# A 4x4 Hadamard convolution as the last of four layers: both directions transformed on the data, the two output halves in two strips of array columns, the data planes shared by VectorE and GpSimd

## The chip, the cores and the metric

One Trainium2 chip, one core. The kernel computes four convolution layers in one launch. The metric is the time of one execution on the device in microseconds (us); lower is better. Engines are named as the profile names them: PE is TensorE (PEld its weight loads), DVE is VectorE, ACT is ScalarE, POOL is GpSimd, SP is SyncE, which here only issues transfers.

## The reference, cut to what matters

All data is float32, `x` has the shape (2, 128, 128, 128): batch, channels, rows, columns. Each layer normalises its input in 32 groups of channels and adds its result to the input. The change touches the last layer only:

```python
_HMT  = [[1,1,1,1],[1,-1,1,-1],[1,1,-1,-1],[1,-1,-1,1]];  _HMT2 = _HMT[[1,0,2,3], :]
_IH = (_HMT / 4)[1:3, :];  _IH2 = (_HMT2.T / 4)[1:3, :]

def _L3_conv_ref(x, weight, bias):                 # weight: (128, 128, 4, 4)
    patches = _extract_patches(x)                  # 4x4 patches at stride 2, padding 1
    hmt1 = einsum('up,bchwpq,qv->bchwuv', _H,  patches, _H)
    hmt2 = einsum('pu,bchwpq,qv->bchwuv', _H2, patches, _H2)
    m1 = einsum('bchwuv,ocuv->bohwuv', hmt1, weight[:64])
    m2 = einsum('bchwuv,ocuv->bohwuv', hmt2, weight[64:])
    o1 = einsum('au,bohwuv,cv->bohwac', _IH,  m1, _IH)
    o2 = einsum('au,bohwuv,cv->bohwac', _IH2, m2, _IH2)
    ...                                            # a, c: place in a 2x2 block of the output
    return out + bias

x = x + _L3_conv_ref(_gn(x), weight, bias)
```

Each 4x4 patch is turned into 16 sums and differences (u, v) of its taps, each is multiplied with its own 128 x 64 weights for the first and the second half of the output channels (with different matrices for the two halves), and sums and differences of the 16 products make a 2x2 block of the output.

## The kernel before

The data stays in SBUF for the whole kernel as `res`, channels on partitions. The earlier layers are an attention along one direction (layer 0, which ends in a stage that merges its results into `res`), four scans over lines (layer 1), an offsets' convolution and a deformable convolution (layer 2). They run before `layer3` and are the same in both kernels.

`layer3` first loads the weights (`ta`, on ScalarE's queue), transforms them by four adds of 128x1024 on VectorE (L1673 and L1674), and writes them, scaled and with signs, into `weff`: 32 small scalings on VectorE (L1682) for the first 64 output channels, and 32 on ScalarE (L1686) for the other 64. `group_norm` makes scale and shift.

Then it works through 32 blocks of eight rows (2 images x 16 blocks). For each block:

- `normalise`: two ScalarE operations write the normalised even and odd columns, with one row more above and below, into `col0` and `col1`, each 10 rows x 65 columns. GpSimd clears the edge columns and, at the edges of the image, a row.
- `transform`: eight VectorE adds of 128x640 make four planes `x3` (10 rows x 64) of sums and differences of four neighbouring columns. Only one direction is transformed on the data; the other one lies in the weights.
- `multiply`: 4 planes x 2 outputs c x 4 row taps q = 32 matmuls with 128x128 weights and 256 moving columns, into four PSUM tiles m0 to m3, each with two buffers. The profile shows a float32 matmul as two instructions, so 64 of them a block.
- `finish`: ScalarE takes m3 (with the bias) and m2 out of PSUM into `t` and `s`; four VectorE adds of 64x512 add m0 and m1; two of 128x512 make the sum and the difference of `t` and `s`, and two more add the residual `res`; SyncE's queue then sends the block out.

The order of the work on TensorE, VectorE and ScalarE is written out by hand: the class `InOrder` wraps an engine, and what is issued through it keeps the order of the program. Such instructions all carry the helper's line in the profile, L81, so they are told apart by their tiles. Turn i multiplies block i, finishes block i - 1, normalises block i + 2 and transforms block i + 1. GpSimd isn't wrapped.

Other rows that the prediction names: the stage that merges layer 0 (VectorE and GpSimd each add 128x1024 pieces, `res<-te,res`), the last of layer 1's four scans (`ln`, `v`, `u`, `x1t`, with PSUM tiles `pl`), the addition of two sets of scan weights at L1035, a running sum on GpSimd at L183, and the offsets' convolution at L1234 (PSUM tile `ps_off`), whose inner loop is

```python
for k in range(9):
    for s in range(4):
        nc.tensor.matmul(ps[32 * s : 32 * s + 32], lhsT=woff[:, k, :], rhs=..., ...)
```

where the partitions of the output (32 s to 32 s + 31) say which strip of array columns works.

Of the kernel before, what the change touches and what calls it, by code (L numbers as in the profile page):

```python
# [7 lines left out]
F32 = mybir.dt.float32  # L8
I32 = mybir.dt.int32
AF = mybir.ActivationFunctionType  # L10
ALU = mybir.AluOpType
AX = mybir.AxisListType
PSUM = bass.MemoryType.PSUM
DRAM = bass.MemoryType.DRAM

P = 128
N = 2
S = 128
# [1633 lines left out]
def layer3(env, prm, res, st_gn, out):  # L1652

    nc, tc = env.nc, env.tc
    flip = (1, 0, 2, 3)
    RB = 8
    with ExitStack() as ctx:  # L1660
        cp = ctx.enter_context(tc.tile_pool(name="l3c", bufs=1))
        bias = cp.tile([P, 1], F32, name="bias3", tag="bias3")
        nc.scalar.dma_start(out=bias, in_=prm["b3"])
        weff = cp.tile([P, 4, 2, 4, P], F32, name="weff", tag="weff")
        with tc.tile_pool(name="l3w", bufs=1) as wp:
            ta = wp.tile([P, 16 * P], F32, name="ta", tag="ta")
            tb = wp.tile([P, 16 * P], F32, name="tb", tag="tb")
            nc.scalar.dma_start(out=ta, in_=prm["w3"])
            a, b = ta, tb
            for bit in range(2):  # L1670
                va = a.rearrange("p (h t k) -> p h t k", t=2, k=P << bit)
                vb = b.rearrange("p (h t k) -> p h t k", t=2, k=P << bit)
                nc.vector.tensor_tensor(vb[:, :, 0], va[:, :, 0], va[:, :, 1], ALU.add)  # L1673
                nc.vector.tensor_tensor(vb[:, :, 1], va[:, :, 0], va[:, :, 1], ALU.subtract)  # L1674
                a, b = b, a
            what = a.rearrange("p (u v o) -> p u v o", u=4, v=4)
            for u in range(4):
                for c in range(2):
                    for q in range(4):
                        to = weff[:, u, c, q, :]  # L1680
                        sign = (1, -1, 1, -1)[u]
                        nc.vector.tensor_scalar(  # L1682
                            to[:, 0:64], what[:, u, (c + 1) ^ q, 0:64], sign / 16, None, ALU.mult
                        )
                        sign = (-1, 1, 1, -1)[u] * (-1, 1)[c]
                        nc.scalar.mul(  # L1686
                            to[:, 64:128],
                            what[:, (0, 3, 2, 1)[u], (3, 2)[c] ^ flip[q], 64:128],
                            sign / 16,
                        )  # L1690

        sp = ctx.enter_context(tc.tile_pool(name="l3s", bufs=2))
        with tc.tile_pool(name="l3pn", bufs=1, space=PSUM) as pn:
            gs, gb = env.group_norm(cp, pn, st_gn, "l3")
        pp = ctx.enter_context(tc.tile_pool(name="l3ps", bufs=2, space=PSUM))
        pe, dve, act = (InOrder(tc, e) for e in (nc.tensor, nc.vector, nc.scalar))
        blocks = [(n, h) for n in range(N) for h in range(0, S, RB)]

        def normalise(i):

            n, h = blocks[i]
            lo, hi = max(0, h - 1), min(S, h + RB + 1)
            cols = [
                sp.tile([P, RB + 2, 65], F32, name=f"col{k}", tag=f"col{k}") for k in range(2)
            ]
            nc.gpsimd.memset(cols[0][:, :, 0:1], 0.0)  # L1706
            nc.gpsimd.memset(cols[1][:, :, 64:65], 0.0)  # L1707
            for k in range(2):
                if h == 0:
                    nc.gpsimd.memset(cols[k][:, 0, :], 0.0)  # L1710
                if h == S - RB:
                    nc.gpsimd.memset(cols[k][:, RB + 1, :], 0.0)
            rows = slice(lo - h + 1, hi - h + 1)
            for k in range(2):
                act.activation(
                    cols[k][:, rows, 1 - k : 65 - k],
                    res[n][:, lo:hi, 1 - k :: 2],
                    AF.Identity,
                    bias=gb[:, n : n + 1],
                    scale=gs[:, n : n + 1],  # L1720
                )
            return cols

        def transform(cols):

            x = sp.tile([P, 4, RB + 2, 64], F32, name="x3", tag="x3")
            t = sp.tile([P, 2, RB + 2, 64], F32, name="t3", tag="t3", bufs=1)
            for k, op in ((0, ALU.add), (2, ALU.subtract)):
                even, odd = x[:, k], t[:, k // 2]
                dve.tensor_tensor(even, cols[0][:, :, 0:64], cols[0][:, :, 1:65], op)  # L1730
                dve.tensor_tensor(odd, cols[1][:, :, 0:64], cols[1][:, :, 1:65], op)
                dve.tensor_tensor(x[:, k + 1], even, odd, ALU.subtract)
                dve.tensor_tensor(even, even, odd, ALU.add)
            return x

        def multiply(x):
            got = []
            for u in range(4):
                ps = pp.tile([P, 2, RB // 2, 64], F32, name=f"m{u}", tag=f"m{u}")
                for c in range(2):  # L1740
                    for q in range(4):
                        pe.matmul(
                            ps[:, c],
                            lhsT=weff[:, u, c, q, :],
                            rhs=x[:, u, q : q + RB - 1 : 2, :],
                            start=(q == 0),
                            stop=(q == 3),
                        )
                got.append(ps.rearrange("p c h w -> p (c h w)"))
            return got  # L1750

        def finish(i, m):

            n, h = blocks[i]
            t = sp.tile([P, 512], F32, name="t", tag="t")
            s = sp.tile([P, 512], F32, name="s", tag="s")
            act.activation(t, m[3], AF.Identity, bias=bias)
            act.copy(s, m[2])
            for half, k in ((slice(0, 64), (0, 1)), (slice(64, 128), (1, 0))):
                dve.tensor_tensor(t[half], m[k[0]][half], t[half], ALU.add)  # L1760
                dve.tensor_tensor(s[half], m[k[1]][half], s[half], ALU.add)
            ot = sp.tile([P, RB, S], F32, name="ot", tag="ot")
            o = ot.rearrange("p (h a) (w c) -> p a c h w", a=2, c=2)
            r = res[n][:, h : h + RB, :].rearrange("p (h a) (w c) -> p a c h w", a=2, c=2)
            tv = t.rearrange("p (c h w) -> p c h w", c=2, w=64)
            sv = s.rearrange("p (c h w) -> p c h w", c=2, w=64)
            for a, op in enumerate((ALU.add, ALU.subtract)):
                dve.tensor_tensor(o[:, a], tv, sv, op)
                dve.tensor_tensor(o[:, a], o[:, a], r[:, a], ALU.add)
            nc.sync.dma_start(out=out[n, :, h : h + RB, :], in_=ot)  # L1770

        count = len(blocks)
        cols = {0: normalise(0), 1: normalise(1)}
        xs = {0: transform(cols.pop(0))}
        ms = {}
        for i in range(count + 1):
            if i < count:
                ms[i] = multiply(xs.pop(i))
            if i >= 1:
                finish(i - 1, ms.pop(i - 1))  # L1780
            if i + 2 < count:
                cols[i + 2] = normalise(i + 2)
            if i + 1 < count:
                xs[i + 1] = transform(cols.pop(i + 1))

# [3 lines left out]
def program(ctx, tc, prm, out):  # L1791
# [32 lines left out]
    with tc.tile_pool(name="l1w", bufs=1) as wp:  # L1824
# [3 lines left out]
        layer1(env, prm, res, both, x1_d, st_gn[1], st_gn[0], first)  # L1828
    layer2(env, prm, res, mem, tables, st_gn[0], st_gn[1])
    layer3(env, prm, res, st_gn[1], out)  # L1830


# [127 lines left out]
```

## Time and profile before

| | |
|---|---|
| median of 3 runs | 5747.52 us (5745.45 to 5751.23) |
| the profiled execution | 5755.18 us, its span 5753.0 us |
| mean granted TensorE clock | 0.97 |
| PE busy | 5381.7 us (94%) |
| DVE busy | 3775.1 us (66%) |
| ACT busy | 2647.0 us (46%) |
| POOL busy | 1288.8 us (22%) |
| last layer: issue of its first load, first matmul, start of the last eviction | 5279.86, 5298.18, 5742.68 us |

How to read the rows: a group's row has the line, the engine, the operation, the tiles written and read, the shapes and the count; then the busy time in us and the mean length of one in ns; then the idle time of the engine just before these instructions, and what ended most of it. In a timeline a row begins with its start and length in us. Busy times of matmuls overlap, since the engine takes up the next before the last has ended; the pace is busy time by count. In a row of a tile the three numbers after the count are the shortest, the median and the longest in ns. A VectorE operation's length reaches a little into the next one's; the distance of two starts is its price in a stream.

### The profile page before, as it was taken

The page shows a single profiled execution, that of the slowest core. Times are in us where ns is not written, and L with a number is a line of the kernel's source. Part 1 is how long each engine was busy: PE and PEld are TensorE (multiplying, and loading weights), DVE is VectorE, ACT ScalarE, POOL GpSimd, SP SyncE. Part 2 cuts the span into 40 slices and gives each one's busy share as a digit, 9 for nine tenths or more (in the row PEclk, how much of TensorE's full clock was granted, in tenths as well). Part 3 has the DMA queues.
Part 4 walks back from the last instruction along what each step waited for, and adds up shares of the span by engine and source line. Part 5 has one row for each costly group of instructions (what it writes and reads, how often), then busy time and mean ns, then how long its engine had stood idle before and what let it go on. Part 6 is the DMA issues. An engine that isn't in the chain of part 4 may idle for free. (4 is left out here: it accounts for less than half of the span.)

```text
span 5753.0 us, 162512 instructions
## 1 busy us (share of the span) xinstructions
PE 5381.7 (94%) x67323; PEld 4838.1 (84%) x67323; DVE 3775.1 (66%) x7289; ACT 2647.0 (46%) x7928; POOL 1288.8 (22%) x983
## 2 busy tenths in 40 slices
PE   8997999999999708999999999997999999998999
PEld 8866888888888608999999999963999999998888
DVE  3645888888888765555555566643666666666887
ACT  1046989898888774442223320022333333333221
POOL 2113666666666530000000013310000000000000
PEclk9998999999999859999999999998999999999999
DMA  3243333333333491000000001125766677663001
GB/s 146 96 189 105 62 62 60 59 62 62 59 59 58 125 373 50 2 1 1 1 1 1 1 16 39 44 65 118 87 88 88 87 84 90 88 87 50 41 37 41
DMA packets 413668, 401.01 MB, mean 70 GB/s; under 512 B 63488, under 2 KB 368512, under 8 KB 402304
## 3 DMA queue, kind: packets, MB, share of 16 engines
q1 hardware_dynamic: 403856, 363.87, 30.9%
q10 hardware_dynamic: 9072, 26.64, 1.2%
q8 instruction: 541, 8.86, 0.7%
q14 instruction: 199, 1.63, 0.1%
HBM read 251.00 MB, written 139.37 MB: 68 GB/s over the span
## 5 line engine op out<-in xcount | busy, mean ns | idle before, releaser
L81 PE MATMUL pl<-ln,wl 128*128 128x128 f32 (+1 forms) x10160 | 1240.7, 276 | 7.4 <-DVE ln L81 7.2
L81 PEld LDWEIGHTS pl<-ln,wl 128*128 128x128 f32 x10160 | 1176.2, 190 | 18.3 <-DVE ln L81 4.4
L81 ACT ACTIVATE e<-e,mx 128x128 f32<-128x128 f32 x2048 | 793.4, 395 | 0.8 <-DVE mx L81 0.8
L81 ACT COPY sm<-ps_s 128x432 f32<-128x432 f32 (+1 forms) x768 | 318.3, 487 | 803.3 <-PE ps_s L81 803.3
L81 ACT COPY res<-ln 128x128 f32<-128x128 f32 x762 | 262.0, 344 | 720.4 <-DVE ln L81 720.4
L81 POOL TENSOR_TENSOR e<-e,total 128x1024 f32<-128x1024 f32 x256 | 485.9, 1898 | 478.1 <-DVE total L81 470.3
L81 DVE COPY s<-ps_w 100x1152 f32<-100x1152 f32 x256 | 346.5, 1354 | 307.1 <-PE ps_w L81 307.1
L81 PE MATMUL ps_s<-s,xw 100*128 100x144 f32 x4096 | 545.1, 286 | 0.2 <-ACT sm L81 0.2
L81 PE MATMUL po<-sm,wdef 128*128 128x256 f32 x2304 | 539.1, 379 | 0.0
L81 PE MATMUL pl<-ln,ws 128*128 128x128 f32 x4064 | 536.8, 273 | 0.0
L81 POOL COPY et<-et 128x1024 f32<-128x1024 f32 x256 | 516.1, 2016 | 35.7 <-DVE et L81 27.0
L81 PEld LDWEIGHTS ps_s<-s,xw 100*128 100x128 f32 x4096 | 517.1, 190 | 0.7 <-ACT sm L81 0.7
L81 DVE TENSOR_TENSOR v<-pl,c 128x128 f32<-128x128 f32 x508 | 148.2, 292 | 538.0 <-PE pl L81 538.0
L81 PEld LDWEIGHTS pl<-ln,ws 128*128 128x128 f32 x4064 | 494.5, 190 | 0.0
L81 ACT ACTIVATE r<-gen,alphas 128x1536 f32<-128x1536 f32 x256 | 394.9, 1543 | 174.2 <-PE gen L81 145.3
L81 POOL TENSOR_TENSOR res<-ln,x1t 128x128 f32<-128x128 f32 x256 | 134.4, 525 | 1485.1 <-DVE ln L81 1485.1
L81 PEld LDWEIGHTS po<-sm,wdef 128*128 128x128 f32 x2304 | 419.8, 190 | 47.6
L81 PE MATMUL m<-x,weff 128*128 128x256 f32 x2048 | 444.4, 380 | 14.8 <-DVE x L81 14.8
L81 PEld LDWEIGHTS m<-x,weff 128*128 128x128 f32 x2048 | 390.6, 191 | 68.3 <-issue 14.9
L1706 POOL MEMSET col<- 128x10 f32 x32 | 3.7, 116 | 1869.1 <-ACT weff L1686 1490.7
L81 ACT ACTIVATION_READ_ACCUMULATOR e<-e,mx 128x1 f32 x2048 | 396.7, 194 | 0.0
L81 DVE SCALAR_TENSOR_TENSOR ln<-v,res 128x128 f32<-128x128 f32 x1016 | 343.7, 338 | 49.2 <-DVE v L81 1.3
(225 smaller groups left out, 8806.6 us busy)
## 6 DMA issues: line engine op xcount, KB each, us to landing
xw<-px_d SPq DMA_DIRECT2D x1280, 80.0 KB
xa<-in_x SPq DMA_DIRECT2D x16, 1024.0 KB
v_d<-vs SPq DMA_DIRECT2D x16, 1024.0 KB
qb_d<-sb SPq DMA_DIRECT2D x16, 1024.0 KB
qa_d<-sa SPq DMA_DIRECT2D x8, 2048.0 KB
zz<-qb_d SPq DMA_DIRECT2D x1024, 16.0 KB
vt<-v_d SPq DMA_DIRECT2D x64, 256.0 KB
qk<-qa_d SPq DMA_DIRECT2D x256, 64.0 KB
```

The lines of the kernel that those rows point to most:

```text
L81: return lambda *a, **k: self.tc.keep_in_program_order(issue(*a, **k))
L1706: nc.gpsimd.memset(cols[0][:, :, 0:1], 0.0)
```

## The change

Both directions are now transformed on the data, separately for the two halves of the output channels, and each matmul has 64 output channels.

- Weights: ScalarE scales `ta` by 1/16 as a whole; VectorE makes `tb` and then `weff` by 16 adds of 128x256.
- `normalise`: the same; GpSimd's memsets keep the program's order now (`pool` is wrapped too).
- `second`, on GpSimd: planes for the second half: two adds of 650 elements (even and odd columns) into `a3`, two of 650 (even and odd rows) into `b3`.
- `first_columns`, on VectorE: four adds of 640 elements into `d3`. `first_rows`: four adds of 1024 elements into `q3`, three on VectorE and one on GpSimd.
- `multiply`: 2 x 2 x 2 x 2 products x 2 halves = 32 matmuls with 128x64 weights and 256 moving columns; the halves alternate, and write partitions 0 to 63 and 64 to 127 of one PSUM tile `m3` with three buffers.
- `combine`: ScalarE takes half of `m3` out of PSUM (two operations of 256 elements, one with the bias); VectorE adds and subtracts the other half in PSUM (two of 512 elements), then makes sums and differences of the result (two of 512) into `ot`.
- `finish`: GpSimd adds the residual (1024 elements); SyncE's queue sends the block out.
- Buffers: `a3`, `d3`, `c3` and `f3` have one, `b3`, `ot` and the columns two, `q3` four, which is one block's planes.
- Order: turn i multiplies block i; then finishes block i - 2 and makes the planes of block i + 1; then combines block i - 1 and normalises block i + 2.

The diff, cut to its core:

```diff
-        weff = cp.tile([P, 4, 2, 4, P], F32, name="weff", tag="weff")
+        weff = cp.tile([P, 4, 4, P], F32, name="weff", tag="weff")
...
+            nc.scalar.mul(ta, ta, 1.0 / 16)
+            def pairs(engine, to, w):
+                one, two = slice(0, H), slice(H, P)
...
+            pairs(nc.vector, lambda k, o: tb[:, k, :, o], lambda v, o: ta[:, :, v, o])
+            pairs(nc.vector, lambda k, o: weff[:, :, k, o], lambda u, o: tb[:, :, u, o])
...
-        pp = ctx.enter_context(tc.tile_pool(name="l3ps", bufs=2, space=PSUM))
-        pe, dve, act = (InOrder(tc, e) for e in (nc.tensor, nc.vector, nc.scalar))
+        pp = ctx.enter_context(tc.tile_pool(name="l3ps", bufs=3, space=PSUM))
+        pe, dve, act, pool = (
+            InOrder(tc, e) for e in (nc.tensor, nc.vector, nc.scalar, nc.gpsimd)
+        )
...
+        def second(cols):
+            even, odd = cols
+            a = sp.tile([P, 2, RB + 2, 65], F32, name="a3", tag="a3")
+            b = sp.tile([P, 2, 2, RB // 2 + 1, 65], F32, name="b3", tag="b3", bufs=2)
+            for k, op in enumerate((ALU.subtract, ALU.add)):
+                pool.tensor_tensor(a[:, k], even, odd, op)
+            for k, op in enumerate((ALU.subtract, ALU.add)):
+                pool.tensor_tensor(b[:, k], a[:, :, 0::2, :], a[:, :, 1::2, :], op)
+            return b
+
+        def first_columns(cols):
+            even, odd = cols
+            d = sp.tile([P, 4, RB + 2, H], F32, name="d3", tag="d3")
+            for k, op in enumerate((ALU.add, ALU.subtract)):
+                dve.tensor_tensor(d[:, 2 * k], odd[:, :, 0:H], even[:, :, 1:65], op)
+                dve.tensor_tensor(d[:, 2 * k + 1], even[:, :, 0:H], odd[:, :, 1:65], op)
+            return d
+
+        def first_rows(d, k):
+            q = sp.tile([P, 4, RB // 2, H], F32, name="q3", tag="q3", bufs=4)
+            lo, hi = ((1, 2), (0, 3))[k % 2]
+            (dve, dve, dve, pool)[k].tensor_tensor(
+                q,
+                d[:, :, lo : lo + RB - 1 : 2, :],
+                d[:, :, hi : hi + RB - 1 : 2, :],
+                ALU.add if k < 2 else ALU.subtract,
+            )
+            return q
+
+        def multiply(qs, b):
+            ps = pp.tile([P, 2, 2, RB // 2, H], F32, name="m3", tag="m3")
+            for r in range(2):
                 for c in range(2):
...
+                    for x in range(2):
+                        for y in range(2):
+                            for half in range(2):
+                                part = slice(H * half, H * half + H)
+                                if half == 0:
+                                    rhs = qs[2 * r + x][:, 2 * c + y]
+                                else:
+                                    rhs = b[:, r, c, x : x + RB // 2, y : y + H]
+                                pe.matmul(
+                                    ps[part, r, c],
+                                    lhsT=weff[:, 2 * r + x, 2 * c + y, part],
+                                    rhs=rhs,
+                                    start=(x == 0 and y == 0),
+                                    stop=(x == 1 and y == 1),
+                                )
+            return ps
+
+        def combine(ps):
+            c = sp.tile([P, 2, RB // 2, H], F32, name="c3", tag="c3")
+            act.activation(c[:, 0], ps[:, 0, 0], AF.Identity, bias=bias)
+            act.copy(c[:, 1], ps[:, 0, 1])
...
+            for k, op in enumerate((ALU.add, ALU.subtract)):
+                dve.tensor_tensor(
+                    f[:, k].rearrange("p c h w -> p (c h w)"),
+                    c.rearrange("p c h w -> p (c h w)"),
+                    ps[:, 1].rearrange("p c h w -> p (c h w)"),
+                    op,
+                )
+            for k, op in enumerate((ALU.add, ALU.subtract)):
+                dve.tensor_tensor(o[:, k], f[:, :, 0], f[:, :, 1], op)
+            return ot
+
+        def finish(i, ot):
             n, h = blocks[i]
...
+            pool.tensor_tensor(ot, ot, res[n][:, h : h + RB, :], ALU.add)
             nc.sync.dma_start(out=out[n, :, h : h + RB, :], in_=ot)
+
+        def transform(i, cols, ots):
+            if i - 3 in ots:
+                finish(i - 3, ots.pop(i - 3))
+            if i >= count:
+                return None
+            b = second(cols)
+            d = first_columns(cols)
+            return [first_rows(d, k) for k in range(4)], b
...
+        planes = {0: transform(0, cols.pop(0), ots)}
+        for i in range(count + 3):
             if i < count:
+                ms[i] = multiply(*planes.pop(i))
+            planes[i + 1] = transform(i + 1, cols.pop(i + 1, None), ots)
+            if i - 1 in ms:
+                ots[i - 1] = combine(ms.pop(i - 1))
             if i + 2 < count:
                 cols[i + 2] = normalise(i + 2)
```

More of the change, by code (lines that the diff above doesn't have):

```diff
@@ L1657, in layer3 @@
     nc, tc = env.nc, env.tc
-    flip = (1, 0, 2, 3)
     RB = 8
+    H = 64
     with ExitStack() as ctx:
@@ L1663, in layer3 @@
         nc.scalar.dma_start(out=bias, in_=prm["b3"])
-        weff = cp.tile([P, 4, 2, 4, P], F32, name="weff", tag="weff")
+        weff = cp.tile([P, 4, 4, P], F32, name="weff", tag="weff")
         with tc.tile_pool(name="l3w", bufs=1) as wp:
[L1666 to L1690, printed above, removed]
@@ L1692, in layer3 @@
-        sp = ctx.enter_context(tc.tile_pool(name="l3s", bufs=2))
+            ta = wp.tile([P, 4, 4, P], F32, name="ta", tag="ta")
+            tb = wp.tile([P, 4, 4, P], F32, name="tb", tag="tb")
+            nc.scalar.dma_start(out=ta.rearrange("p u v o -> p (u v o)"), in_=prm["w3"])
+            nc.scalar.mul(ta, ta, 1.0 / 16)
+            def pairs(engine, to, w):
+                one, two = slice(0, H), slice(H, P)
+                for k, (a, b, op) in enumerate(
+                    ((0, 3, ALU.add), (0, 3, ALU.subtract), (2, 1, ALU.add), (2, 1, ALU.subtract))
+                ):
+                    engine.tensor_tensor(to(k, one), w(a, one), w(b, one), op)
+                for k, (a, b, op) in enumerate(
+                    ((3, 1, ALU.subtract), (3, 1, ALU.add), (2, 0, ALU.subtract))
+                ):
+                    engine.tensor_tensor(to(k, two), w(a, two), w(b, two), op)
+                nc.vector.scalar_tensor_tensor(
+                    to(3, two), w(2, two), -1.0, w(0, two), ALU.mult, ALU.subtract
+                )
@@ L1693, in layer3 @@
+            pairs(nc.vector, lambda k, o: tb[:, k, :, o], lambda v, o: ta[:, :, v, o])
+            pairs(nc.vector, lambda k, o: weff[:, :, k, o], lambda u, o: tb[:, :, u, o])
+        sp = ctx.enter_context(tc.tile_pool(name="l3s", bufs=1))
         with tc.tile_pool(name="l3pn", bufs=1, space=PSUM) as pn:
             gs, gb = env.group_norm(cp, pn, st_gn, "l3")
-        pp = ctx.enter_context(tc.tile_pool(name="l3ps", bufs=2, space=PSUM))
-        pe, dve, act = (InOrder(tc, e) for e in (nc.tensor, nc.vector, nc.scalar))
+        pp = ctx.enter_context(tc.tile_pool(name="l3ps", bufs=3, space=PSUM))
@@ L1703, in normalise @@
             cols = [
-                sp.tile([P, RB + 2, 65], F32, name=f"col{k}", tag=f"col{k}") for k in range(2)
-            ]
-            nc.gpsimd.memset(cols[0][:, :, 0:1], 0.0)
-            nc.gpsimd.memset(cols[1][:, :, 64:65], 0.0)
+                sp.tile([P, RB + 2, 65], F32, name=f"col{k}", tag=f"col{k}", bufs=2)
+                for k in range(2)
+            ]
+            pool.memset(cols[0][:, :, 0:1], 0.0)
+            pool.memset(cols[1][:, :, 64:65], 0.0)
             for k in range(2):
                 if h == 0:
-                    nc.gpsimd.memset(cols[k][:, 0, :], 0.0)
+                    pool.memset(cols[k][:, 0, :], 0.0)
                 if h == S - RB:
-                    nc.gpsimd.memset(cols[k][:, RB + 1, :], 0.0)
+                    pool.memset(cols[k][:, RB + 1, :], 0.0)
             rows = slice(lo - h + 1, hi - h + 1)
@@ L1722, in normalise @@
             return cols
[L1724 to L1739, printed above, removed]
-                for c in range(2):
[L1741 to L1750, printed above, removed]
@@ L1752, in finish @@
-        def finish(i, m):
-            n, h = blocks[i]
[L1755 to L1769, printed above, removed]
-            nc.sync.dma_start(out=out[n, :, h : h + RB, :], in_=ot)
+        def second(cols):
[7 more added lines that the diff above has]
+            return b
@@ new lines, in combine @@
+        def combine(ps):
+            c = sp.tile([P, 2, RB // 2, H], F32, name="c3", tag="c3")
+            act.activation(c[:, 0], ps[:, 0, 0], AF.Identity, bias=bias)
+            act.copy(c[:, 1], ps[:, 0, 1])
+            f = sp.tile([P, 2, 2, RB // 2, H], F32, name="f3", tag="f3")
+            ot = sp.tile([P, RB, S], F32, name="ot", tag="ot", bufs=2)
+            o = ot.rearrange("p (h a) (w c) -> p a c h w", a=2, c=2)
+            for k, op in enumerate((ALU.add, ALU.subtract)):
[4 more added lines that the diff above has]
+                    op,
+                )
+            for k, op in enumerate((ALU.add, ALU.subtract)):
+                dve.tensor_tensor(o[:, k], f[:, :, 0], f[:, :, 1], op)
+            return ot
@@ L1772, in layer3 @@
         count = len(blocks)
         cols = {0: normalise(0), 1: normalise(1)}
-        xs = {0: transform(cols.pop(0))}
-        ms = {}
-        for i in range(count + 1):
+        ots, ms = {}, {}
+        planes = {0: transform(0, cols.pop(0), ots)}
+        for i in range(count + 3):
             if i < count:
-                ms[i] = multiply(xs.pop(i))
-            if i >= 1:
-                finish(i - 1, ms.pop(i - 1))
+                ms[i] = multiply(*planes.pop(i))
+            planes[i + 1] = transform(i + 1, cols.pop(i + 1, None), ots)
+            if i - 1 in ms:
+                ots[i - 1] = combine(ms.pop(i - 1))
@@ L1781, in layer3 @@
             if i + 2 < count:
                 cols[i + 2] = normalise(i + 2)
-            if i + 1 < count:
-                xs[i + 1] = transform(cols.pop(i + 1))
 @with_exitstack
```

## The prediction

> **What bounds the kernel now.** I read the page's slices first, then the groups of the last layer by form, then the timeline and the sums by stretch of that layer, and at last every row of the earlier layers in which GpSimd adds. The last layer is a stage by itself: its first matmul starts at 5298.18 us and the span ends at 5753.0.
>
> ```profile
> 5310.00:5743.00 433.00, 432.60 (x2005) 380.48 (x2003) 350.37 (x488) 86.47 (x121) 7.45 (x62) 1.00 0.09 38
> ```
>
> The columns of this sum over a stretch are the length, then busy time and count of PE, PEld, DVE, ACT and POOL, the granted clock, the DMA share and GB/s. TensorE is busy for 432.6 of 433.0 us at full clock: the stage ends when TensorE ends. VectorE is at 81%, GpSimd nearly idle.
>
> ```profile
> L81 PE MATMUL m<-x,weff 128*128 128x256 f32 x2048 | 444.4, 380 | 14.8 <-DVE x L81 14.8
> L81 POOL TENSOR_TENSOR res<-te,res x16: 2359/3422/3447, 2012.6 to 2158.6; 128x1024 f32<-128x1024 f32 x16
> L1234 PE MATMUL ps_off<-gx,woff 128*32 128x512 f32 x1152 | 130.3, 605 | 4.3 <-ACT gx L1222 4.3
> L1035 POOL TENSOR_TENSOR ws<-wl 128x512 f32<-128x512 f32 x4 | 5.1, 1268 | 22.0 <-DVE gs_l L44 11.3 <-DMA wl<-in_wscan 10.7
> ```
>
> The first row gives the period: 444.4 / 32 blocks = 13.89 us a block, in which 32 written matmuls appear as 64 recorded ones, 217 ns each (444.4 / 2048). The other three price what the change adds.
>
> **Part by part: TensorE.** The change writes again 32 matmuls of 256 columns a block, but each with 64 output channels, alternating between two strips of array columns. If strips don't overlap, a block still costs 64 x 217 ns = 13.9 us; if they overlap fully, 6.9 us. The nearest row is the offsets' convolution (ps_off), which alternates between four strips of 32 columns: 130.3 us / 1152 = 113 ns for 512 moving columns, where the full-width matmul of layer 0 with 512 (ps_q) takes 61.4 us / 128 = 480 ns. Four strips give a factor 4.2, so I take the full factor 2: 6.9 us. TensorE stops being the bound.
>
> **ScalarE.** Two normalisations at 0.98 us stay; the two evictions (0.69 and 0.58 us) halve in size. Under 3.3 us a block, hidden.
>
> **VectorE.** It now has 16 operations a block, 11.2 us (350.37 / 433 x 13.89). Starts of neighbours give the price of one in a stream: 0.73 us for 640 elements (5301.08 to 5301.81), 1.14 for the 1024-element adds of the weights (5287.52 to 5288.66), 0.61 for 512 (5318.50 to 5319.11). Afterwards: four adds of 640 in first_columns (2.92), three of 1024 in first_rows (3.42), two of 512 with one operand in PSUM and two in SBUF in combine (4 x 0.65 = 2.6): 8.9 us. Nine of these eleven have both inputs in SBUF; only the two with a PSUM input don't.
>
> **GpSimd.** It gets, a block, four adds of 650 elements (second), one of 1024 (the fourth plane), one of 1024 (the residual in finish) and its two memsets of 0.12 us. The rows above give 1.268 us for 512 and 2.36 us for 1024 undisturbed (the 2359 minimum), so 2.13 ns an element; 650 costs 1.268 + 138 x 2.13 ns = 1.56 us. Sum: 4 x 1.56 + 2 x 2.36 + 0.24 = 11.2 us, of which 10.96 are adds. The other end for the rate is 1.75 ns an element, which the 128x2286 add at L183 shows (3998 ns), with both reads from one tile shifted by one element; the new adds read other planes or rows, like the 2.13 rows, so I take 2.13.
>
> **The two together.** If they ran side by side, GpSimd's 11.2 us would be the new period and the kernel faster. But the residual add of the merge stage says otherwise:
>
> ```profile
> 2012.63 4.68 POOL L81 TENSOR_TENSOR res<-te,res 128x1024 f32<-128x1024 f32 x2 [24.29 <-DMA res<-in_x]
> ...
> 2034.14 1.23 DVE L81 TENSOR_TENSOR res<-te,res 128x1024 f32<-128x1024 f32 x1
> 2034.19 3.42 POOL L81 TENSOR_TENSOR res<-te,res 128x1024 f32<-128x1024 f32 x1 [16.88 <-DVE te L81]
> ```
>
> Two adds of 128x1024 with VectorE idle take 4.68 us. The same add begun 0.05 us after a VectorE add with two SBUF inputs takes 3.42; so it goes in 14 of the 16 (the tile's row above: minimum 2359, median 3422). It grows by 1.07 us, which is nearly all of what VectorE's add has left, while that add keeps its 1.23 us. The small adds of layer 1's last pass agree, and show which partners matter:
>
> ```profile
> 3604.74 0.28 DVE L81 TENSOR_TENSOR u<-pl,c 128x128 f32<-128x128 f32 x1
> 3604.90 0.47 POOL L81 TENSOR_TENSOR res<-ln,x1t 128x128 f32<-128x128 f32 x1 [1.61 <-DVE ln L81]
> ...
> 3605.94 0.29 DVE L81 TENSOR_TENSOR ln<-ln,ln 128x128 f32<-128x128 f32 x1
> 3605.99 0.58 POOL L81 TENSOR_TENSOR res<-ln,x1t 128x128 f32<-128x128 f32 x1 [0.62 <-DVE ln L81]
> ```
>
> Beside an add that reads PSUM (pl) GpSimd takes 0.47 us, beside one that reads SBUF twice (ln, ln) 0.58: 0.1 us more for 128 elements, as 1.07 for 1024. So GpSimd makes no progress while VectorE reads two SBUF inputs, 1.04 ns an element, and these times add up. In the new block such VectorE adds have 4 x 640 + 3 x 1024 + 2 x 512 = 6656 elements: 6.95 us. Period: 6.95 + 10.96 = 17.9 us.
>
> Bounds. Below: GpSimd's fixed part may lie beside VectorE's reads. The two prices give 1.268 - 512 x 0.00213 = 0.18 us fixed, six times 1.1 us, so 16.8 us; with the 1.75 ns rate (4648 elements, 8.1 us) 15.1. Above: VectorE's nine adds count at their price in a stream, 2.92 + 3.42 + 1.22 = 7.6, so 18.5 us, plus about 0.1 us at each of some ten handovers (0.09 from the end of VectorE's te at 2034.10 to GpSimd's start at 2034.19), 19.5. What the trace doesn't show is GpSimd first and VectorE second: there VectorE may wait, or GpSimd may be interrupted; both sum to the same. [...]
>
> Waits that the change adds: d3 has one buffer, so VectorE's first_columns of the next block waits for GpSimd's fourth plane; behind it are queued first_rows and combine. GpSimd's finish waits for combine of two blocks earlier, and behind it are queued second and the fourth plane, for which TensorE waits. The single sets of q3 let planes be written only once the last block's matmuls have read them. With 6.9 us of matmuls in 17.9 these waits fall beside the two busy engines; I cost them at nothing. If TensorE drops to half clock (0.56 was granted from 5280 to 5298 us, where it was idle), its 13.9 us are still covered by 17.9. [...]
>
> **The edges.** Weights: four adds (start-to-start 1.15 us) and 32 + 32 small scalings give way to one scaling on ScalarE, about 2.0 us (a 1536-element one takes 1.54), and 16 adds of 256 elements on VectorE, 0.35 us each on the line through 0.61 for 512 and 1.14 for 1024, 5.6 us. The first normalisation no longer queues behind 32 scalings, so it starts at about 5288 and not 5293.61; but second then lies beside those 16 adds. The first matmul needs b and the first plane: 5297 to 5304 against 5298.2. I add 3 us. The end: after the last matmul 10.3 us now; afterwards some 0.8 + 2.6 + 2.4 and the same 4.2 us of output, 10.0. Nothing.
>
> **Sum.** 32 x (17.9 - 13.89) = +128, +3: +131 us. The profiled execution took 5755.18 us (span 5753.0), the median of the runs is 5747.52; 5755.2 + 131 = 5886 for a profiled one, 5879 for the median.
>
> **Rivals.**
> Side by side: GpSimd and VectorE don't hold each other up in this mix. GpSimd bounds, 11.2 us and about 0.3 of gaps: 32 x (11.5 - 13.89) + 3 = -73, 5674. For it: the big GpSimd operations of the attention run at full speed beside VectorE. Against it: those partners read PSUM or one input, and the 14 of 16. It decides if the period of adds side by side falls below 13.89, that is if under 2.7 us of VectorE's 6.95 delay GpSimd.
>
> Only a start waits: a GpSimd add waits for the VectorE add that runs as it begins, then both go on freely. Six waits of half a VectorE add (6.95 / 9 / 2 = 0.39) to a whole one (0.77): 13.5 to 15.8, say 14.2 us, +13: 5760. For it: every stretched row began just after VectorE's. Against it: a GpSimd add longer than the next VectorE adds has no row at all.
>
> No overlap of strips: TensorE keeps 13.9 us. Alone it would mean no change, 5748; under the forecast it is hidden. Against it: ps_off's 113 ns.
>
> **Chances.** The adds exclude each other 0.83; side by side 0.11; only starts wait, or strips without overlap with no exclusion, 0.06 (half of it within 0.2%, half slower). Differences of 0.2%, about 11 us, are what a measurement of this kernel can tell from none. Faster 0.11, same 0.03, slower 0.86. The forecast's own range is 15.1 us (+39, so 5789 with the edges) to 19.5 us and 5 us of edges (+185, 5932). That leaves out the 0.11, the 0.06 and little else.
>
> **What would show it.** Right: a period of 17 to 19 us between output DMAs; POOL busy 80% or more, with its adds of 650 at 2 us and more and those of 1024 near 3; TensorE's row near 110 ns a matmul at full clock, idle more than half the time, clock under 1. Wrong: GpSimd's adds at 1.56 and 2.36 us and a period near 11.5; or TensorE still busy throughout.

## The result and the profile after

The changed kernel takes 5873.31 us (median of 4 runs, 5870.9 to 5885.79) against 5746.49 us before: the ratio is 1.0225, with a 95% interval of 1.0207 to 1.0243. The profiled execution took 5885.79 us, its span is 5883.9. That is 130.9 us more span than before, and it divides so: the last layer's first load is issued at 5283.16 us and not 5279.86 (+3.3, in layers that the change doesn't touch); from there to the first matmul 23.9 us and not 18.3 (+5.6); from the first to the last matmul 564.5 us and not 444.0 (+120.5); behind it 12.3 us and not 10.8 (+1.5).

The sum over nearly all of the last layer, with the columns as before (length, then busy time and count of PE, PEld, DVE, ACT, POOL, granted clock, DMA share, GB/s):

```profile
5310.00:5870.00 560.00, 303.44 (x2024) 171.07 (x2026) 555.49 (x339) 74.07 (x120) 446.09 (x250) 0.73 0.07 28
```

TensorE fell from always busy to 54%. VectorE stands at 99%, GpSimd at 80%. Between the starts of the fifth and the 29th output transfer a block takes 18.23 us, before 13.81. The groups of this stretch, by form:

```profile
L81 PE MATMUL m<-q,weff 128*64 128x256 f32 x1012 | 302.2, 463 | 257.5 <-DVE q L81 257.5
L81 DVE TENSOR_TENSOR q<-d 128x1024 f32<-128x1024 f32 x95 | 244.0, 2619 | 3.2
L81 DVE TENSOR_TENSOR d<-col,col 128x640 f32<-128x640 f32 x124 | 242.5, 2014 | 0.3
...
L81 POOL TENSOR_TENSOR a<-col,col 128x650 f32<-128x650 f32 x62 | 132.8, 2165 | 0.1
L81 POOL TENSOR_TENSOR b<-a 128x650 f32<-128x650 f32 x62 | 126.5, 2059 | 2.4
L81 POOL TENSOR_TENSOR q<-d 128x1024 f32<-128x1024 f32 x31 | 103.3, 3333 | 3.1 <-DVE d L81 3.1
L81 POOL TENSOR_TENSOR ot<-ot,res 128x1024 f32<-128x1024 f32 x29 | 83.1, 2865 | 104.6 <-DVE ot L81 104.6
```

Two rows of the kernel before, with the lengths of VectorE's adds there:

```profile
L81 DVE TENSOR_TENSOR x<-col 128x640 f32<-128x640 f32 x64 | 52.4, 818 | 1.5 <-POOL col L1710 1.5
...
L1673 DVE TENSOR_TENSOR ta<-tb 128x1024 f32<-128x1024 f32 x1 | 1.2, 1225 | 0.0
```

VectorE's adds of 640 elements took 0.82 us in the kernel before and now take 2.01; those of 1024 took 1.22 in the weights' transform and now 2.62. GpSimd's add of 1024, 2.36 us undisturbed, takes 2.87 and 3.33. So both engines' adds got longer, and the busy shares of both contain waiting. The timeline shows how; first two adds in the middle of the stage, then three rows near its end:

```profile
5498.60 3.33 POOL L81 TENSOR_TENSOR q<-d 128x1024 f32<-128x1024 f32 x1
5499.64 3.37 DVE L81 TENSOR_TENSOR q<-d 128x1024 f32<-128x1024 f32 x1
...
5870.11 2.36 POOL L81 TENSOR_TENSOR ot<-ot,res 128x1024 f32<-128x1024 f32 x1 [3.68 <-DVE ot L81]
5870.16 1.28 DVE L81 TENSOR_TENSOR f<-c,m 128x512 f32<-128x512 f32 x2
...
5871.54 2.08 DVE L81 TENSOR_TENSOR ot<-f 128x512 f32<-128x512 f32 x2
```

GpSimd's plane ends at 5501.93. VectorE's plane starts 1.04 us after GpSimd's and ends 1.08 us after GpSimd's end: it waited for GpSimd's whole add and then did its own. In the last three rows GpSimd runs its undisturbed 2.36 us beside two VectorE adds that read PSUM (`m`), 0.64 us each as ever; the pair that follows reads SBUF alone (`f`), and takes 2.08 us instead of 1.30, since its first one lasts beyond GpSimd's end at 5872.47.

### The profile page after: what moved, and what is told of

Its sections match the earlier page's. It is cut to its first block, busy times and chain, and to the rows that moved or that the text cites. A ratio compares the mean times of both kernels' runs of the same rounds, so it can differ in the third digit from the quotient of the medians.

```text
span 5883.9 us, 162468 instructions
## 1 busy us (share of the span) xinstructions
PE 5248.5 (89%) x67323; PEld 4624.8 (79%) x67323; DVE 3977.2 (68%) x7109; ACT 2630.3 (45%) x7897; POOL 1746.9 (30%) x1175
## 5 line engine op out<-in xcount | busy, mean ns | idle before, releaser
L81 PEld LDWEIGHTS pl<-ln,wl 128*128 128x128 f32 x10160 | 1176.6, 190 | 18.2 <-DVE ln L81 4.4
L81 PE MATMUL m<-q,weff 128*64 128x256 f32 x1024 | 305.9, 463 | 278.1 <-DVE q L81 278.1
L81 PEld LDWEIGHTS m<-q,weff 128*64 128x64 f32 x1024 | 163.3, 167 | 412.1 <-issue 301.1
```

The lines of the kernel that those rows point to most:

```text
L81: return lambda *a, **k: self.tc.keep_in_program_order(issue(*a, **k))
```

## The experiments

The theory is the prediction's: a GpSimd add and a VectorE add with both inputs in SBUF exclude each other, so their times add up. The rivals: the waits on single buffers and between the engines' queues make the 18.2 us; the engines run side by side and something else is slow; any VectorE add hinders GpSimd, whatever it reads. Each run's time stands against runs of the kernel before on the same chip. In the eight profiles the last layer's first load is issued between 5267.8 and 5283.2 us, though the layers ahead of it are the same; so a time can be off by some 10 us that aren't the last layer's, and the period of a block (from the fifth to the 29th output transfer) is the safer figure.

**The second engine's adds given to the first.**

```diff
-                pool.tensor_tensor(a[:, k], even, odd, op)
+                dve.tensor_tensor(a[:, k], even, odd, op)
...
-                pool.tensor_tensor(b[:, k], a[:, :, 0::2, :], a[:, :, 1::2, :], op)
+                dve.tensor_tensor(b[:, k], a[:, :, 0::2, :], a[:, :, 1::2, :], op)
...
-            (dve, dve, dve, pool)[k].tensor_tensor(
+            dve.tensor_tensor(
...
-            pool.tensor_tensor(ot, ot, res[n][:, h : h + RB, :], ALU.add)
+            dve.tensor_tensor(ot, ot, res[n][:, h : h + RB, :], ALU.add)
```

Expected: 

> All of GpSimd's adds in the last layer go to VectorE (GpSimd keeps its memsets); nothing else changes. Theory (an add of GpSimd and a VectorE add with two SBUF inputs exclude each other, in both directions): giving the second engine's work to the first makes the layer faster. VectorE has 4 x 0.73 + 4 x 1.14 + 4 x 0.74 + 1.14 + 4 x 0.65 = 14.2 us a block in a stream, 14.5 with the waits between dependent adds, against the measured 18.2 of the changed kernel: about 5760 us, 5745 to 5790; VectorE's adds of 640 at 0.82 us and of 1024 at 1.22 again. Rival (the waits on single buffers and between the engines' queues set the 18.2 us, not the adds themselves): the chain stays and VectorE gets 5.3 us more, 18 us or more, 5870 and up.

Measured: 5757.21 us, 1.0023 of the kernel before (1.0013 to 1.0032); 14.64 us a block.

```profile
L81 DVE TENSOR_TENSOR q<-d 128x1024 f32<-128x1024 f32 x87 | 100.8, 1220 | 2.3
L81 DVE TENSOR_TENSOR d<-col,col 128x640 f32<-128x640 f32 x88 | 66.5, 819 | 0.0
```

With GpSimd out of the way, VectorE's adds have their old lengths, and from its first load to the end the layer takes 486.9 us instead of 600.8: 114 us less by using one engine less. The buffers and the order of the work are those of the changed kernel, so single buffers alone didn't make the 18.2 us. The waits between VectorE and GpSimd are gone with GpSimd's adds, so on those this run decides nothing; the next two, which keep both engines at work, do.

**Less for GpSimd to do.** The planes of the second half are a constant.

```diff
-            b = second(cols)
+            b = b0
```

Expected: 

> Leaves out the four adds of 650 elements for the second half (its planes are a constant); GpSimd keeps the fourth plane and the residual, 4.7 us a block. Theory (the times add up): VectorE's two-input adds 6.95 us and GpSimd's 4.7 make at least 11.7 us; with the 1.3 us of VectorE's adds out of PSUM, in which GpSimd waits for their result, 13.0; so 12.6 us a block, about 5694 us, 5670 to 5715. Rival (side by side, the 18.2 us come from second's adds being slow by themselves): VectorE's 8.9 us bound, about 5590 us. Rival (waits between the queues): no less than 17 us a block, 5835 and up.

Measured: 5722.24 us, 0.9959 (0.9946 to 0.9971); 13.39 us a block.

```profile
L81 DVE TENSOR_TENSOR q<-d 128x1024 f32<-128x1024 f32 x72 | 135.6, 1937 | 2.5
L81 DVE TENSOR_TENSOR d<-col,col 128x640 f32<-128x640 f32 x97 | 127.6, 1374 | 0.0
```

Taking 5.9 us of GpSimd's adds away took 4.8 us off the block; side by side the block would have taken 8.9 us, and with the waits as the cause 17 or more. The time lies 7 us above the expected range, and the block 0.8 us above the expected 12.6. The rows give it as VectorE's own 8.9 us and what GpSimd's two adds put on top: the four adds of 640 are longer by 0.55 us each (1.37 against 0.82), the three of 1024 by 0.72 (1.94 against 1.22), 2.2 us and 2.2 us, together 13.3. GpSimd's `finish` starts only when `combine` is over, so nothing of it lies beside the 1.3 us in which VectorE reads PSUM.

**One input of first_columns from PSUM.** ScalarE writes the odd columns once more, into PSUM.

```diff
+        def in_psum(i):
...
+            act.activation(odd[:, lo - h + 1 : hi - h + 1, 0:64], res[n][:, lo:hi, 0::2], AF.Identity, ...)
+            return t, odd
...
-            even, odd = cols
+            even, odd = cols[0], op3[1]
```

Expected: 

> ScalarE writes the odd columns a second time, into PSUM, and first_columns reads them there, so its four adds have one SBUF input; the products' PSUM tile has two buffers and not three. Same adds, same engines. Theory (only VectorE adds with two SBUF inputs exclude GpSimd): first_columns lies beside GpSimd's adds; GpSimd's run of about 10 us, three planes of VectorE that alternate with it (3.2) and combine (2.6) make 15.8 us a block: about 5795 us, 5775 to 5815; its adds of 640 near 0.8 us instead of 2.0. Rival (any VectorE add slows GpSimd's, whatever it reads): 18.2 us as before, 5873. Rival (waits): 5873 too.

Measured: 5783.45 us, 1.0064 (1.0041 to 1.0088); 15.13 us a block.

```profile
L81 DVE TENSOR_TENSOR q<-d 128x1024 f32<-128x1024 f32 x64 | 140.5, 2246 | 2.3
...
L81 POOL TENSOR_TENSOR a<-col,col 128x650 f32<-128x650 f32 x44 | 68.6, 1583 | 11.6 <-ACT col L81 11.6
L81 POOL TENSOR_TENSOR ot<-ot,res 128x1024 f32<-128x1024 f32 x21 | 49.8, 2370 | 23.4 <-DVE o L81 23.4
...
L81 DVE TENSOR_TENSOR d<-col,o 128x640 f32<-128x640 f32 x44 | 35.7, 811 | 0.0
L81 DVE TENSOR_TENSOR d<-o,col 128x640 f32<-128x640 f32 x43 | 35.3, 821 | 41.1 <-ACT col L81 41.1
```

```profile
5508.10 2.37 POOL L81 TENSOR_TENSOR ot<-ot,res 128x1024 f32<-128x1024 f32 x1 [0.88 <-DVE o L81]
...
5510.17 0.82 DVE L81 TENSOR_TENSOR d<-o,col 128x640 f32<-128x640 f32 x1 [1.88 <-ACT col L81]
...
5511.05 3.15 POOL L81 TENSOR_TENSOR a<-col,col 128x650 f32<-128x650 f32 x2 [0.59 <-ACT col L81]
```

The same adds on the same engines: `d`, with one input from PSUM (`o`), is back at 0.81 and 0.82 us, and the GpSimd adds `a` that now lie beside it take 1.58 us instead of 2.17. The planes `q`, still with two SBUF inputs, stay at 2.25 us. So it is what VectorE reads that counts. GpSimd's `ot` at 2.37 us says less, since VectorE is idle for most of it. ScalarE's added operation was not hidden: VectorE waits 41.1 us in 21 blocks, 2.0 us each, until ScalarE has written the odd and then the even columns, which it can start only when VectorE has cleared the PSUM tile's edge behind `combine`. The expectation had no such wait, so that its range held is in part luck; the lengths of the adds carry the argument.

**The planes' odd rows in PSUM as well.** VectorE makes all four planes, each from rows in SBUF and rows in PSUM; `first_columns` becomes eight adds of 320 elements.

```diff
+            do = op3[0][:, 650:1930].rearrange("p (k h w) -> p k h w", k=4, w=H)
+            for r, d in ((1, do), (0, de)):
...
+                    dve.tensor_tensor(d[:, 2 * k], odd[:, r::2, 0:H], even[:, r::2, 1:65], op)
...
+            one, two = (d[x % 2][:, :, x // 2 : x // 2 + RB // 2, :] for x in (lo, hi))
+            dve.tensor_tensor(q, one, two, ALU.add if k < 2 else ALU.subtract)
```

Expected: 

> As the run with the odd columns in PSUM, and the odd rows of first_columns' result also lie in PSUM, so that first_rows' adds have one SBUF input too; VectorE makes all four planes; GpSimd keeps second and the residual. Theory (two SBUF inputs): of VectorE's adds only combine's last two still exclude GpSimd's; VectorE bounds with 8 x 0.43 + 4 x 1.14 + 2.6 = 10.6 us, 11.0 with waits: about 5642 us, 5620 to 5700, faster than both kernels. If TensorE, with idle gaps, falls to half clock for most of its matmuls, 13.9 us: 5735. Rival (any VectorE add excludes GpSimd's): 10.6 + 7.6 us a block, 5870.

Measured: 5718.49 us, 0.9949 (0.9931 to 0.9967), 18 us above the expected range; 13.18 us a block, not 11.0. The exclusion was gone (`q` at 1.21 and 1.22 us), but the waits, of which this row names VectorE's own, show that the hole of the run before has stayed:

```profile
DVE o L81 <- ACT col L81: 46.9, 24, 2.0
```

The odd columns' PSUM tile has one buffer, and its clearing stood behind `combine` on VectorE, ScalarE's write behind that. VectorE was idle for 46.9 us in 24 blocks, 2.0 us each.

**The odd columns earlier, and where they don't block.** The PSUM tile is taken once, its zero column cleared once, and ScalarE writes right behind `first_columns`.

```diff
+        t3 = qp.tile([P, 1930], F32, name="o3", tag="o3")
+        nc.vector.memset(t3[:, 0:650], 0.0)
...
             d = first_columns(cols, o3.pop(i))
+            if i + 1 < count:
+                o3[i + 1] = in_psum(i + 1)
```

Expected: 

> As the run with the planes in PSUM, but the PSUM tile is kept for good, so its zero column is cleared once, and ScalarE writes the next block's odd columns as soon as first_columns has read the last ones, not after combine. In the run before, VectorE stood idle for 2.0 us a block waiting for that write. Theory (VectorE's own stream is the bound once its adds don't exclude GpSimd's): 13.18 - 2.0 = 11.2 us a block, 8 x 0.49 + 4 x 1.14 + 2.6 = 11.1 by its parts: 32 x 2.0 = 64 us less than 5718, about 5655 us, 5640 to 5680. Rival (adds out of PSUM still hold up GpSimd, and the idle time only hid it): 13 us a block, 5715.

Measured: 5689.11 us, 0.9898 (0.9881 to 0.9914), 9 us above the expected range; 12.10 us a block. Half of the hole had moved: `first_rows` reads the same tile and now waited for the write.

```profile
DVE q L81 <- ACT o L81: 28.3, 26, 1.4
```

So the last run keeps the tile but issues the write behind `combine`, as in the run before that one.

```diff
-            if i + 1 < count:
-                o3[i + 1] = in_psum(i + 1)
...
+                o3[i + 2] = in_psum(i + 2)
                 cols[i + 2] = normalise(i + 2)
```

Expected: 

> As the run with the early odd columns, but ScalarE's write of the next block's odd columns is issued behind combine again; the PSUM tile stays for good. In the run before, VectorE waited 1.1 us a block at first_rows for that write, since both lie in one tile. Theory (VectorE's stream of 11.1 us is the bound): 12.10 - 1.1 = 11.0 us a block, 32 x 1.1 = 35 us less than 5689: about 5655 us, 5640 to 5670. Rival (the write moves to another place on VectorE's path, as behind combine before, where 2.0 us were lost): 12 to 13 us a block, 5685 to 5718.

Measured: 5674.6 us, 0.9883 of the kernel before (0.9866 to 0.9899): 1.2% faster than the kernel before, and faster than the changed one. A block takes 11.52 us, half a microsecond more than expected, and the time lies 5 us above the range. With no edge to clear behind `combine`, ScalarE's write waits for `first_rows`' reads alone:

```profile
ACT o L81 <- DVE q L81: 199.0, 25, 8.3
```

The sum over 320 us of the stage, columns as above:

```profile
5330.00:5650.00 320.00, 229.05 (x1790) 168.45 (x1788) 297.83 (x445) 93.93 (x140) 227.92 (x202) 0.90 0.11 45
```

And two of its groups by form:

```profile
L81 POOL TENSOR_TENSOR b<-a 128x650 f32<-128x650 f32 x56 | 74.6, 1353 | 2.2
L81 DVE TENSOR_TENSOR q<-d,o 128x1024 f32<-128x1024 f32 x56 | 67.7, 1210 | 0.0
```

VectorE is busy for 93% with adds of undisturbed length, GpSimd for 71% beside it, and `b` takes 1.35 us instead of 2.06.

## Why the prediction was right, point by point

- **TensorE.** Right. At full clock (1.00 granted from 5502 to 5507 us) two matmuls of the two strips start every 0.21 to 0.22 us (5502.18, 5502.40, 5502.61), 108 ns each against 217 before, the full factor 2, and the rival without overlap falls. The strips' gain is real, but TensorE was then no longer what the stage waited for: it waited for VectorE's planes for 257.5 of 560 us.
- **The exclusion.** Right, and in both directions. The trace of before had only the case in which VectorE came first. Now VectorE's plane, begun second, waits for GpSimd's whole add (5499.64 to 5501.93) and takes 3.37 us, 1.22 in the one-engine run. With one input in PSUM neither engine was held up: `d` at 0.81 us beside GpSimd's `a` at 1.58. The rivals fall with that: side by side by VectorE's 2.01 and 2.62 us against 0.82 and 1.22 in the one-engine run, and the one in which only GpSimd's start waits by VectorE's 3.37 us.
- **The period.** 17.9 predicted, 18.23 measured, with errors that nearly cancel. GpSimd's adds of 650 elements cost 1.58 (`a`) and 1.35 us (`b`) undisturbed, not 1.56 both, which makes 0.4 us less a block. The 1.3 us of VectorE's adds out of PSUM were taken to lie beside GpSimd's adds. They don't: GpSimd stands idle for 104.6 us in 29 blocks, 3.6 us each, until `combine` has ended. Some 2.4 of these are the end of VectorE's last plane and its adds out of SBUF, which exclude GpSimd anyway; the rest are those 1.3 us. The prediction named that wait and costed it at nothing, as one that falls beside two busy engines; but GpSimd isn't busy in it. What then remains, 17.9 - 0.4 + 1.3 - 18.23 = 0.6 us, would be GpSimd's fixed parts beside VectorE's reads, which the lower bound had allowed for; no run measured that by itself. The 18.5 us of whole instructions, which the prediction worked out as well, lie about as near.
- **From period to stage.** The prediction multiplied by 32. But 32 x 18.23 = 583.4 us, and the matmuls took 564.5. The first two blocks start 13.62 and 13.74 us before the next (5307.10, 5320.72, 5334.46 us) and the third 17.21, since `combine` and `finish` aren't at work yet: 10.1 us less. The last block's matmuls need 9.5 us and not a whole period, since TensorE isn't the bound: 8.7 us less. The longer period gave 32 x 0.33 = 10.6 back. So that the profiled time met the forecast's 5886 us to the microsecond is luck: -18.9 and +10.6 here, +3.3 in layers that the change doesn't touch, +2.6 and +1.5 at the edges nearly cancel.
- **The edges.** +3 predicted for the start, +5.6 measured. The prediction had the first normalisation at 5288 us, freed from the 32 scalings. It starts at 5295.90, after a wait for the last of the weights' adds, so it didn't get ahead of them. That its tiles take over memory of the weights' is an explanation that was only argued. The end cost 1.5 us and not nothing.
- **The clock.** TensorE's granted clock fell to 0.73, with gaps of up to 9.1 us. Behind the gap of 8.1 us that ends at 5497.57 a pair of matmuls takes 0.42 to 0.43 us (5500.26 to 5500.69; 0.51 granted from 5497.6 to 5502 us) before it takes 0.21 (1.00 from 5502 to 5507 us). As predicted this cost nothing: VectorE, busy for 555.5 of 560 us, didn't wait for TensorE.

## What to carry to other kernels

Before adds are shared between VectorE and GpSimd, ask of every VectorE add whether both its inputs are in SBUF. For the float32 adds of this kernel, its time and that of the GpSimd adds with SBUF inputs beside it then added up (3.37 us for a plane of VectorE behind one of GpSimd's, 1.22 alone), and since GpSimd takes about twice as long (2.36 us against 1.22 for 1024 elements), the sharing lost: 18.23 us a block against 14.64 on VectorE alone. An input in PSUM lifted that (`d` 0.81 us and not 2.01): with the odd columns and the planes' odd rows in PSUM, the fourth plane moved to VectorE and a wait on the PSUM tile taken out, a block took 11.52 us. How much of that the moved plane gave, no run shows. And when one engine's share of the work is halved, price the period of the next one from rows in which that engine has its new neighbours.

## What the runs showed of the hardware that was not expected

- Where VectorE waits for GpSimd's add it is recorded as busy: it shows 99% in the changed kernel, of which the one-engine run's lengths (0.82 and 1.22 us against 2.01 and 2.62) leave less than half as work for `d` and `q`.
- GpSimd's add of 650 elements took 1.58 us from two tiles and 1.35 us from alternating rows of one tile in the last run, where VectorE's adds for the planes have an input in PSUM.
- VectorE's adds cost the same with one input in PSUM: 0.81 and 0.82 us for 640 elements against 0.82 with both in SBUF in the one-engine run, 1.21 and 1.22 for 1024 against 1.22.
